# Second half's tokens normed one tile at a time during the first half and kept in DRAM, with inputs loaded and inner sums made at other steps, in a float32 decoder layer on one core

## The chip, the core and the metric

The kernel runs on one core of a Trainium2 chip. The metric is device time in microseconds (us), the median of three runs: 1939.29 us for the kernel before (1936.71 to 1942.11). Everything is float32. The engines are TensorE (PE in the profile; PEld is its weight load), VectorE (DVE), ScalarE (ACT), GpSimd (POOL) and SyncE (SP), which here issues nearly all the DMAs.

## What is computed

A decoder layer on 2048 tokens of width 512: attention with 32 heads of 128, cross attention to a small context, and a bias mixture of 64 experts, each behind a layer norm without weights and each added to its input. Only the first part matters here:

```python
def _layernorm(x, axis=-1, eps=1e-05):
    m = jnp.mean(x, axis=axis, keepdims=True)
    v = jnp.var(x, axis=axis, keepdims=True)
    return (x - m) / jnp.sqrt(v + eps)
...
q = (hidden_states @ Wq + bq).reshape(b, n, H, HD)
k = (hidden_states @ Wk + bk).reshape(b, n, H, HD)
v = (hidden_states @ Wv + bv).reshape(b, n, H, HD)
q = rmsnorm(q, gq)
k = rmsnorm(k, gk)
scores = jnp.einsum('bnhd,bmhd->bhnm', q, k) * scale
attn = jax.nn.softmax(scores.astype(jnp.float32), axis=-1).astype(q.dtype)
out = jnp.einsum('bhnm,bmhd->bnhd', attn, v).reshape(b, n, H * HD)
return out @ Wo + bo
...
x = x + _L0_attn_ref(_layernorm(x, axis=-1), ...)
```

There are 32 sequences of 64 tokens, so attention stays inside a sequence.

## The kernel before, in words

**Tokens.** The 2048 tokens are 16 tiles of 128 (NT), 8 pairs of tiles (NPAIR), 4 quads of 4 tiles (NQUAD), 2 halves of 8 tiles. A pair is an `AttentionInput` (L272): its constructor loads the two tiles (L283), `norm` (L285) takes their mean and variance (`statistics`, L216: L222 and L223 on VectorE for each tile, then the inverse root on ScalarE, L229 and L230, or on GpSimd, L226 and L227) and puts the two subtract-and-scale steps (L289, VectorE) on the list `waiting`. `turn` (L294) transposes the pair on TensorE into PSUM banks of the pool ps_s (three banks, which the scores, the mix and the sums of squares use too) and writes blocks for a Strassen product: three copies on ScalarE (L312 to L314), two sums on VectorE (L315, L316), two on GpSimd (L317, L318).

**Heads.** The 32 heads are 16 groups of two (NHG). The main loop (L1235) runs over 32 steps, for each half all 16 groups. The projections use Strassen's seven products in place of eight. In the first group of a half the two quads are handled one after the other (`single`, L1183, with `HeadGroup.project`, L419): these are the first and the second unit. In the 15 other groups both quads are taken together (`double`, L1194, with `Window`, L609): here Strassen's scheme is used twice, which needs, for each of seven outer products o, four more sums of the half's blocks: `inner_input` (L324), two on VectorE (L328, L329), then two on GpSimd (L330, L331). They are made once for each half.

**Weights.** `Weights` (L91) loads a group's Wq, Wk and Wv in six DMAs of 256 KB (L107). `prepare` loads those of the next group; their own Strassen sums (L120 on VectorE for the very first group, else on GpSimd; L152 to L155 on GpSimd) are made step by step by `make`.

**The order of the work.** Inside the attention part the orders of TensorE, VectorE, ScalarE and GpSimd are those of the program (`manual_schedule`, L67 and L1100): an instruction waits for all that the program put ahead of it on its engine. SyncE is not listed there; the framework orders its DMAs itself, except those of `load` (L212). The program is therefore a hand-written interleaving. `project` of a unit yields 14 times (steps 1 to 14), and `single` calls what is listed for a step (L1185, and the table `between` of the caller). A window has four groups n of outer products, (1, 5), (2, 6), (7, 3) and (4), with four steps m each, and `double` has a plan for each (n, m): `v` does a piece of the value projection, `line.scale` multiplies queries and keys of an earlier unit by their inverse root mean squares (L527 on GpSimd, L529 on VectorE; the factors come by a broadcast DMA, L518, into one of two buffers tagged rsb), `line.turn` and `line.attend` do scores, softmax (L254 to L262), mix (L577) and its store (L592, L599). Nearly each step also takes one entry from `waiting`.

**What TensorE waits for.** Products accumulate in PSUM banks. A partial result must be read by VectorE before the next product goes on in its bank: L445 and L450 in a unit, L651, L661 and L664 in a window (some by ScalarE, L654 and L388). Such a read is called a keep below.

**Where the norms and sums stand before the change.** At the start pairs 0 and 1 are loaded and normed; `turn` of each loads the pair two further on (L320). In the first group, `coming[0].norm()` (L1240) stands ahead of the first unit; pair 2 (in the second half 6) is turned after step 6 and pair 3 (7) after step 11. The second unit makes the inner sums 1 and 5 after steps 2 and 4, the first window 2, 6, 7, 3 and 4 after (0, 0), (0, 2), (1, 0), (1, 2) and (2, 1). In the last window of the first half pairs 4 and 5 are loaded into the two rsb buffers after (2, 1) and (2, 2), normed by `norms` (L1289) ahead of that window's last softmax, and turned after it.

## Time and profile before

| | |
|---|---|
| median of three runs | 1939.29 us |
| the profiled execution: its time | 1943.95 us |
| the profiled execution: its span, first to last instruction | 1942.2 us |
| mean granted TensorE clock | 0.989 |
| attention of the first half | 10 to 705 us |
| attention of the second half | 705 to about 1400 us |
| output projection, cross attention, experts | from about 1400 us |

The profile page lists busy time by engine, then the span in 40 slices, the DMA queues, the chain of work that ended last, and the costliest groups of instructions. A row of the timeline gives start, duration, engine, line of the kernel, operation, output and input; in brackets stands how long the engine had been idle before it, and what ended that. A DMA row (SPq) is the issue, not the transfer. The granted clock is TensorE's, as a share of full speed; the column DMA is the mean busy share of the 16 DMA engines.

Durations that recur, from the timeline: statistics of one tile L222 0.66 to 0.70 us and L223 0.18, inverse root on ScalarE 0.30 and 0.20, on GpSimd 0.23 to 0.43 and 0.71 to 0.86, subtract-and-scale L289 0.49 to 0.55, L328 0.37 to 2.00, L329 0.41 to 2.03, L330 0.72 to 1.18, L331 0.72 to 1.18.

### The profile page before, as it was taken

Reading aid. Unit: us, or ns where it says so; the run is one execution under the profiler, and the core shown is the slowest. Engines: PE = TensorE matmul, PEld = TensorE weight load, DVE = VectorE, ACT = ScalarE, POOL = GpSimd, SP = SyncE. Lnnn points to the kernel's source line nnn. Section 1 sums busy time; section 2 is a strip of 40 time slices with the busy share of each in tenths; the row PEclk is TensorE's granted clock in tenths of the full one; section 3 lists DMA queues with packets and bytes.
Section 4 is the critical chain, followed back from the end, with each engine's and each line's share of the span. In section 5 each row is a group of like instructions: output and inputs, shape, how many; then the busy total and the mean of one; then the engine's idle time right before and its main releaser. Section 6 shows DMA issues by size and latency. Waiting matters only on the chain.

```text
span 1942.2 us, 40532 instructions
## 1 busy us (share of the span) xinstructions
PE 1891.5 (97%) x16877; PEld 1628.0 (84%) x16877; DVE 1211.4 (62%) x2024; ACT 643.6 (33%) x1567; POOL 1046.5 (54%) x816
## 2 busy tenths in 40 slices
PE   8999999999999999999999999999998999999997
PEld 7888888888888878888888888888887888888875
DVE  5766767766667667766666666666545445554545
ACT  2244334344433443334433333443311112221122
POOL 4865667665567548666557666655225323332320
PEclk9999999999999999999999999999999999999998
DMA  4234333333433343333443333344933232223100
GB/s 132 66 99 129 123 111 109 110 99 117 131 125 100 109 141 101 101 107 99 127 133 113 110 109 100 99 130 135 300 118 128 90 106 70 69 90 112 49 20 22
DMA packets 162264, 210.72 MB, mean 108 GB/s; under 512 B 9888, under 2 KB 134880, under 8 KB 157984
## 3 DMA queue, kind: packets, MB, share of 16 engines
q1 hardware_dynamic: 160896, 207.05, 33.1%
q8 instruction: 133, 2.18, 0.5%
q10 hardware_dynamic: 1184, 1.08, 0.2%
q14 instruction: 51, 0.42, 0.1%
HBM read 169.82 MB, written 38.27 MB: 107 GB/s over the span
## 4 chain that ended last, share of the span: by engine, by line
PE 76%; DVE 11%; POOL 7%; issue 3%; DMA 2%; ACT 1%; SPq 0%; POOLq 0%; DVEq 0%; ACTq 0%
PE p_w L640 24%; PE py L822 18%; PE va L372 7%; PE vb L372 6%; POOL qk L719 5%; PE s L540 3%; PE ms_w L764 3%; PE o L577 3%; DVE qk L651 3%; DVE qk L664 3%; PE pa L430 1%; PE pt_p L246 1%; DVE qk L529 1%; DVE sums L259 1%; PE e_x L998 1%
## 5 line engine op out<-in xcount | busy, mean ns | idle before, releaser
L640 PE MATMUL p_w<-x,w 128*128 128x256 f32 x2940 | 726.0, 384 | 13.1 <-DVE qk L651 8.9
L640 PEld LDWEIGHTS p_w<-x,w 128*128 128x128 f32 x2940 | 522.3, 191 | 76.0 <-DVE qk L651 15.5
L651 DVE TENSOR_TENSOR qk<-p_w,qk 128x512 f32<-128x512 f32 x360 | 213.0, 599 | 148.6 <-PE p_w L640 113.0
L341 ACT ACTIVATE sq<-qk 128x512 f32<-128x512 f32 x256 | 158.2, 629 | 397.4 <-POOL qk L719 227.2
L372 PEld LDWEIGHTS va<-w,x 128*128 128x128 f32 x2048 | 265.3, 192 | 28.6 <-ACT v L388 18.3
L372 PE MATMUL va<-w,x 128*128 128x128 f32 x2048 | 277.2, 279 | 0.5 <-ACT v L388 0.5
L822 PE MATMUL py<-wo,a 128*128 128x256 f32 x1152 | 262.5, 381 | 0.0
L664 DVE TENSOR_TENSOR qk<-p_w,qk 128x512 f32<-128x512 f32 x360 | 219.7, 619 | 58.8 <-PE p_w L640 55.3
L120 POOL TENSOR_TENSOR w<-w 128x768 f32<-128x768 f32 x126 | 247.2, 1973 | 2.4
L822 PEld LDWEIGHTS py<-wo,a 128*128 128x128 f32 x1152 | 213.9, 190 | 35.6 <-issue 7.3
L262 POOL TENSOR_TENSOR prob<-prob,inv 128x512 f32<-128x512 f32 x64 | 76.7, 1198 | 293.5 <-DVE inv L261 292.5
L527 POOL TENSOR_TENSOR qk<-qk,rs 128x512 f32<-128x512 f32 x128 | 169.2, 1322 | 118.7 <-DMA rs<-row_w 98.6
L372 PEld LDWEIGHTS vb<-w,x 128*128 128x128 f32 x1536 | 202.3, 192 | 9.8
L372 PE MATMUL vb<-w,x 128*128 128x128 f32 x1536 | 203.3, 275 | 0.0
L388 ACT COPY v<-va 128x256 f32<-128x256 f32 x256 | 94.8, 370 | 320.5 <-PE va L372 320.4
L529 DVE SCALAR_TENSOR_TENSOR qk<-qk,gqk,rs 128x512 f32<-128x512 f32 x128 | 166.4, 1300 | 11.6 <-DMA rs<-row_w 10.2
L822 PE MATMUL py<-wo_t,a 128*128 128x256 f32 x608 | 142.2, 384 | 0.0
L822 PEld LDWEIGHTS py<-wo_t,a 128*128 128x128 f32 x608 | 114.6, 192 | 16.2 <-issue 0.8
L719 POOL TENSOR_TENSOR qk<-qk 128x512 f32<-128x512 f32 x60 | 90.3, 1504 | 60.6 <-DVE qk L664 58.2
L254 DVE TENSOR_REDUCE mx<-s 128x8 f32<-128x512 f32 x64 | 44.2, 691 | 110.0 <-PE s L540 110.0
L392 DVE TENSOR_TENSOR v<-vb,v 128x256 f32<-128x256 f32 x192 | 80.7, 420 | 47.9 <-PE vb L372 27.3
L592 ACT ACTIVATE ot<-o,bvt 128x256 f32<-128x256 f32 x256 | 99.2, 469 | 2.2 <-PE o L577 2.2
(177 smaller groups left out, 2191.4 us busy)
## 6 DMA issues: line engine op xcount, KB each, us to landing
rs<-row_w SPq DMA_DIRECT2D x120, 512.0 KB
mixed<-ot SPq DMA_DIRECT2D x64, 512.0 KB
a<-mixed SPq DMA_DIRECT2D x32, 1024.0 KB
w<-in_wq_dram SPq DMA_DIRECT2D x64, 256.0 KB
w<-in_wk_dram SPq DMA_DIRECT2D x62, 256.0 KB
w<-in_wv_dram SPq DMA_DIRECT2D x62, 256.0 KB
wo<-in_wo_dram SPq DMA_DIRECT2D x8, 1024.0 KB
x<-in_x_dram SPq DMA_DIRECT2D x28, 256.0 KB
```

Source lines behind the costliest of these rows:

```text
L120: on.tensor_tensor(*(it.rearrange("p c j d -> p (c j) d") for it in (out, a, b)), ALU.subtract)
L341: nc.scalar.activation(sq, of, AF.Square)
L372: nc.tensor.matmul(to[:, j, :], left[i][:, c, j, :], right[i][:, c, 2, :], start=first and j == 0 and c == 0, stop=c == 1, skip_group_chec ...
L388: nc.scalar.copy(self.v[h, ab], what)
L527: nc.gpsimd.tensor_tensor(k, k, rk, ALU.mult)
L529: lambda: nc.vector.scalar_tensor_tensor(q, q, gqk, rq, ALU.mult, ALU.mult)
L592: nc.scalar.activation(ot[:, h, :, b * SEQ : (b + 1) * SEQ], o[b][:, h, :, :], AF.Identity, bias=bvt[:, hg * HG + h : hg * HG + h + 1],)
L640: nc.tensor.matmul(bank[:, s, :], self.w.inner[o][i], inner_x[self.half, o][i], start=first and s == 0, stop=True, skip_group_check=True,)
L651: nc.vector.tensor_tensor(to(t, j), bank, add(t, j), ALU.add)
L664: nc.vector.tensor_tensor(to(t, j), bank, to(t, j), ALU.add)
L719: on.tensor_tensor(qk[to], qk[to], qk[what], ALU.add)
L822: nc.tensor.matmul(py, a[:, g, :], b[g // KH][:, g % KH, :], start=n == 0 and g == 0, stop=n == last and g == NHG - 1,)
```

## The change

Six things:

- A DRAM scratch `normed` holds eight normed tiles. In the first half's third to tenth group (2 to 9), a generator `normed_tile` loads one tile of the second half into a new buffer of its own after step (0, 0), takes its statistics after (0, 3), with the inverse root on ScalarE, and after (1, 2) subtracts and scales it and stores it to the scratch.
- Pairs 4 to 7 are loaded from the scratch; their `norm` does nothing, and `norms` with its step is gone.
- Pairs 2 and 3 are both loaded right after the first weights, into the two rsb buffers, and no longer by `turn` of pairs 0 and 1.
- The norm of pair 2 moves from ahead of the first unit to after its step 3.
- `inner_input` yields between its VectorE and its GpSimd part.
- In the second unit the two parts are called so: 1 after steps 1 and 2, 5 after 3 and 4, and the VectorE part alone of 2, 6 and 7 after 6, 8 and 12. In the first window: GpSimd's part of 2 at (0, 0), of 6 at (0, 1), VectorE's of 3 at (0, 2), GpSimd's of 7 at (1, 0), of 3 at (1, 1), VectorE's of 4 at (1, 2), GpSimd's of 4 at (2, 1). In the listing of the first window, the first call for an o that has not begun makes the VectorE part, the second the GpSimd part.

```diff
@@ -168,6 +168,9 @@
                     7: r[:, 0, 1, :],
                 }
 
+
+    normed = scratch.tile([NT // 2, P, D], F32, tag="normed", name="normed")
+
     def load_x(t, place=None):
         xt = xpool.tile([P, D], F32, tag="x", name=f"x{t}") if place is None else place
         nc.sync.dma_start(out=xt, in_=x_flat[bass.ts(t, P), :])
@@ -275,16 +278,27 @@
 
         def __init__(self, pair, beside=False):
 
-            self.pair, self.beside = pair, beside
+            self.pair = pair
             places = [None, None]
             if beside:
                 both = work.tile([P, 2, 2, QT], F32, tag="rsb", name=f"xs{pair}", bufs=2)
                 places = [both[:, i, :, :].rearrange("p h n -> p (h n)") for i in range(2)]
-            self.xs = [load_x(2 * pair + i, place) for i, place in enumerate(places)]
+            self.xs = []
+            for i, place in enumerate(places):
+                t = 2 * pair + i
+                if t < NT // 2:
+                    self.xs.append(load_x(t, place))
+                else:
+                    if place is None:
+                        place = xpool.tile([P, D], F32, tag="x", name=f"xn{t}")
+                    nc.sync.dma_start(out=place, in_=normed[t - NT // 2, :, :])
+                    self.xs.append(place)
 
         def norm(self):
 
-            for xt, (mean, rstd) in zip(self.xs, statistics(self.xs, f"a{self.pair}", self.beside)):
+            if self.pair >= NPAIR // 2:
+                return
+            for xt, (mean, rstd) in zip(self.xs, statistics(self.xs, f"a{self.pair}")):
                 waiting.append(
                     lambda xt=xt, mean=mean, rstd=rstd: nc.vector.tensor_scalar(
                         xt, xt, mean, rstd, ALU.subtract, ALU.mult
@@ -316,7 +330,7 @@
             nc.vector.tensor_tensor(s1, pt[1][:, 0:2, :], a22, ALU.add)
             nc.gpsimd.tensor_tensor(s2, s1, a11, ALU.subtract)
             nc.gpsimd.tensor_tensor(s4, a12, s2, ALU.subtract)
-            if pair + 2 < NPAIR // 2 or pair >= NPAIR // 2 and pair + 2 < NPAIR:
+            if pair in (NPAIR // 2, NPAIR // 2 + 1):
                 coming.append(AttentionInput(pair + 2))
 
     inner_x = {}
@@ -327,6 +341,7 @@
         x11, x21, x12, x22, s1, s2, s3, s4 = (it[:, bass.ts(k, QT)] for k in range(8))
         nc.vector.tensor_tensor(s1, x21, x22, ALU.add)
         nc.vector.tensor_tensor(s3, x11, x21, ALU.subtract)
+        yield
         nc.gpsimd.tensor_tensor(s2, s1, x11, ALU.subtract)
         nc.gpsimd.tensor_tensor(s4, x12, s2, ALU.subtract)
         inner_x[half, o] = {1: x11, 2: x12, 3: s4, 4: x22, 5: s1, 6: s2, 7: s3}
@@ -1116,6 +1131,7 @@
         )
     coming.append(AttentionInput(1))
     weights[0] = Weights("0_0", 0, (nc.sync, nc.scalar, nc.scalar))
+    coming.extend(AttentionInput(pair, True) for pair in (2, 3))
     load(g2[:, 0:1], gq.unsqueeze(1))
     load(g2[:, 1:2], gk.unsqueeze(1))
     load(bvt, bv_t)
@@ -1123,7 +1139,7 @@
     pt = ps_t.tile([P, 4, P], F32, tag="pt", name="pt_i")
     for i in range(28):
         nc.tensor.transpose(pt[:, i % 4, :], ident, ident)
-    for it in coming:
+    for it in coming[0:2]:
         it.norm()
     while waiting:
         take_waiting()
@@ -1180,6 +1196,14 @@
 
     line = Line()
 
+    def normed_tile(t):
+        xt = load_x(t, work.tile([P, D], F32, tag="xn", name=f"xn{t}", bufs=1))
+        yield
+        ((mean, rstd),) = statistics([xt], f"n{t}")
+        yield
+        nc.vector.tensor_scalar(xt, xt, mean, rstd, ALU.subtract, ALU.mult)
+        nc.sync.dma_start(out=normed[t - NT // 2, :, :], in_=xt)
+
     def single(unit, between):
 
         places = {6: [line.scale], 7: [line.turn], 11: [line.scale]}
@@ -1202,7 +1226,7 @@
             [[v], [v], [v, line.scale], [v]],
             [[v, line.scale], [v, line.turn], [v], [line.attend, line.scale]],
             [[v, line.scale], [v], [v], [v]],
-            [[v], [v], [v, line.turn], [*more.pop((3, -1), ()), end]],
+            [[v], [v], [v, line.turn], [end]],
         ]
         for (n, m), them in more.items():
             plan[n][m].extend(them)
@@ -1237,10 +1261,10 @@
         units = [HeadGroup(hg, 2 * half + t, w) for t in range(2)]
         prepare(n)
         if hg == 0:
-            coming[0].norm()
             single(
                 units[0],
                 {
+                    3: lambda: coming[0].norm(),
                     6: lambda: (coming.pop(0).turn(), coming[0].norm()),
                     11: lambda: coming.pop(0).turn(),
                 },
@@ -1250,16 +1274,24 @@
                 nc.vector.tensor_copy(bqd[:, :, 0::HG], b_0)
                 nc.vector.tensor_tensor(bqd[:, :, 1::HG], b_1, b_0, ALU.subtract)
                 nc.vector.tensor_scalar(gqk, g2[:, 0:1], g2[:, 1:2], HD**-0.5, ALU.mult, ALU.mult)
+            inners = {o: inner_input(half, o) for o in (1, 5, 2, 6, 7, 3, 4)}
+
+            def inner(o):
+                next(inners[o], None)
+
             sums_of_next(n)
             make(1)
             single(
                 units[1],
                 {
-                    2: lambda: inner_input(half, 1),
-                    3: lambda: make(1),
-                    4: lambda: inner_input(half, 5),
-                    6: lambda: make(1),
+                    1: lambda: inner(1),
+                    2: lambda: (inner(1), make(1)),
+                    3: lambda: inner(5),
+                    4: lambda: inner(5),
+                    6: lambda: (make(1), inner(2)),
+                    8: lambda: inner(6),
                     11: lambda: make(2),
+                    12: lambda: inner(7),
                 },
             )
         else:
@@ -1274,8 +1306,20 @@
                 more.setdefault((n, m), []).append(it)
 
             if hg == 1:
-                for at, o in (((0, 0), 2), ((0, 2), 6), ((1, 0), 7), ((1, 2), 3), ((2, 1), 4)):
-                    also(*at, lambda o=o: inner_input(half, o))
+                for at, o in (
+                    ((0, 0), 2),
+                    ((0, 1), 6),
+                    ((0, 2), 3),
+                    ((1, 0), 7),
+                    ((1, 1), 3),
+                    ((1, 2), 4),
+                    ((2, 1), 4),
+                ):
+                    also(*at, lambda o=o: inner(o))
+            if half == 0 and 2 <= hg < 2 + NT // 2:
+                norm = normed_tile(NT // 2 + hg - 2)
+                for at in ((0, 0), (0, 3), (1, 2)):
+                    also(*at, lambda norm=norm: next(norm, None))
             if (hg, half) == (NHG - 1, 0):
 
                 for m in range(2):
@@ -1286,13 +1330,6 @@
                     )
                     also(3, 3, lambda: coming.pop(0).turn())
 
-                def norms():
-                    for it in coming:
-                        it.norm()
-                    while waiting:
-                        take_waiting()
-
-                more[3, -1] = [norms]
             if n + 1 == len(groups):
                 four = four_blocks("wo_0")
                 wo_b = [[load_wo(k, 0, four[2 * k : 2 * k + 2])] for k in range(2)]
```

## The prediction, made before the changed kernel was run

> **What bounds the kernel now.** I read the page first: engine sums and chain of waits.
>
> ```profile
> PE 1891.5 (97%) x16877; PEld 1628.0 (84%) x16877; DVE 1211.4 (62%) x2024; ACT 643.6 (33%) x1567; POOL 1046.5 (54%) x816
> PE 76%; DVE 11%; POOL 7%; issue 3%; DMA 2%; ACT 1%; SPq 0%; POOLq 0%; DVEq 0%; ACTq 0%
> ```
>
> TensorE is the bound nearly everywhere; only time in which it idles, or runs at a lower clock, can be won. The busy-time table by stretches of 4 us finds those places (columns: stretch, then PE, PEld, DVE, ACT, POOL busy, granted clock, DMA share, GB/s):
>
> ```profile
> 16.00:20.00 4.00, 0.00 (x0) 0.00 (x0) 1.88 (x5) 0.21 (x1) 2.91 (x2) 0.91 0.67 244
> 20.00:24.00 4.00, 3.53 (x8) 2.86 (x9) 2.26 (x5) 1.18 (x4) 0.00 (x0) 0.50 0.02 4
> 76.00:80.00 4.00, 2.02 (x10) 1.82 (x11) 4.00 (x4) 0.58 (x1) 4.00 (x3) 1.00 0.00 0
> 696.00:700.00 4.00, 1.45 (x78) 1.25 (x72) 3.32 (x8) 1.11 (x3) 1.52 (x3) 1.00 0.80 250
> 700.00:704.00 4.00, 2.65 (x14) 2.44 (x15) 1.00 (x3) 2.96 (x9) 0.00 (x0) 0.74 0.62 205
> 780.00:784.00 4.00, 1.85 (x13) 1.55 (x11) 4.00 (x5) 0.00 (x0) 4.00 (x4) 0.98 0.00 0
> 784.00:788.00 4.00, 3.55 (x12) 3.20 (x13) 2.39 (x4) 1.11 (x3) 3.84 (x5) 0.50 0.00 0
> ```
>
> Four holes: first unit, first window of each half, turn of the halves. Elsewhere the windows are TensorE's own: from one window's sums of squares to the next it is 42.33 or 42.34 us almost without exception. The timeline tells what each hole waits for (the bracket is the idle before and who ended it):
>
> ```profile
> 12.75 1.81 SPq L173 DMA_DIRECT2D x<-in_x_dram  x4
> 18.05 0.69 DVE L222 BATCH_NORM_STATS2 st_a<-x 128x6 f32<-128x512 f32 x1 [4.05 <-DMA x<-in_x_dram]
> 20.47 3.75 PE L430 MATMUL pa<-x,w 128*128 128x256 f32 x8 [4.52 <-DVE qk L445]
> 73.28 3.76 POOL L120 TENSOR_TENSOR w<-w 128x768 f32<-128x768 f32 x2
> 73.37 2.00 DVE L328 TENSOR_TENSOR x<-x 128x256 f32<-128x256 f32 x1
> 75.30 2.02 DVE L329 TENSOR_TENSOR x<-x 128x256 f32<-128x256 f32 x1
> 77.97 1.99 PE L640 MATMUL p_w<-x,w 128*128 128x256 f32 x8 [2.02 <-DVE qk L651]
> ...
> 700.68 0.63 PE L246 MATMUL pt_a<-ident,xs 128*128 128x128 f32 x4 [3.22 <-DVE prob L255]
> 784.45 2.08 PE L640 MATMUL p_w<-x,w 128*128 128x256 f32 x4 [2.60 <-DVE qk L664]
> ```
>
> At 18 us VectorE stands on the third pair's input, with TensorE's keep (L445) queued behind; at 77 and 784 the keeps stand behind inner sums (L328, L329); at 700 the softmax (L254, L255), whose bank the transposes need, stands behind four norms.
>
> **Terms of the sum**, in the profiled execution (1943.95 us, span 1942.2 and 1.75 around it; 4.66 above the median 1939.29). Each hole is its stretch less the same work without a stall.
>
> *First unit.* From the first product (10.45) to the sums of squares (38.23): 27.78. The second half's second unit takes 22.15 (725.59 to 747.74); less 3.17 of squares, scores and mix and 0.44 of turned probabilities, plus two turns at 0.87, the work is 20.28. The hole is 7.5: 4.52 idle, some 3.0 of half clock. The change moves the norm to the third step and loads its input early. The DMA view has 5.31 MB in the first 22 us; less pair 3's 0.5, pair 2 landed as the last of 4.8 MB at 18.05. Now it is the last of 3.0; at that rate (some 0.305 MB/us from 2.3 on) it lands near 12, an estimate. Its 0.5 MB can hold the second half of the first weights back by 1.6 us; SyncE saw a first-weight load land at 10.7 and their sums started at 12.6, so that is just covered, and a longer delay would be paid one for one. The second weights fall behind 1 MB, 3.4 us later on SyncE's queue; POOL first reads them at 38.5, some 20 us after they land. The two buffers lent to the inputs are free after step 11, before the fetches that use them (42.5). The keep L445 then follows the weight sums (end 14.0), and product 6 runs at 15.95 without a stop. What is late next is the third pair's turn, wanted at 18.9: VectorE has L450 (to 15.8), two statistics 1.62, L392 0.42, tensor_scalar 0.54 (behind POOL's L120 until 18.9), L445 0.66, tensor_scalar 0.54, end near 20.6; less the first tile's transposes 0.44, idle 1.3. I take **-6.0**; ends -7.5 (nothing waits) and -2.8 (input no earlier than now: 2.7 idle and 2 of half clock).
>
> *First window, first half.* End of squares 58.94 to 101.88 is 42.94; a steady window has 40.03 (144.91 to 184.94), 1.09 of it a mix that this one lacks: hole 4.0. The vector parts of five sums were here; three (2, 6, 7) leave, 3 goes where 6 was (no stall there) and 4 where 3 was. At the old place of 7 POOL's L120 stays, but VectorE has nothing to lose to it. POOL's parts stay as many; those of 2 and 6 come a step or two earlier, while it waits for a fetch (4.13 idle before 70.11). The next window still waits 0.35 at its L664: **-3.5**, ends -2 and -4.
>
> *First window, second half.* 748.81 to 795.55 is 46.74 against 40.03: hole 6.7; idle 0.79 (behind 7) and 2.60 (behind 4), the rest half clock. Here a rule weighs. The Trainium skill, "TensorE: Matmul & The Clock Gate", Part 1, puts the clock to half after an idle window of about 3.4 us. By it a hole of 2.60 costs 2.60; the row after it shows a clock of 0.50, and at 77 us 2.02 cost none. By rule the term would be about 3.4 less a rest of 0.4, so -3.0, by row **-6.2**. I take the row; ends -3.0 and -6.7.
>
> *Turn of the halves.* Squares at 692.97 to 725.59: 32.62. Work: 22.15, plus 1.24 for the larger squares, plus four turns 3.48: hole 5.75. Gone are four statistics, four tensor_scalars and POOL's two short pairs. The scores end at 696.36, L254 and L255 (0.69 each) would end at 697.8, and the first transposes go there instead of at 700.68. Late next: the banks of the mix, freed by ScalarE's L592 (four, 1.55, begin 698.5 instead of 701.10), then the copies; the first product at 701.5 instead of 704.59, so -3.1, and 0.4 for its half clock. The remaining gaps are under 1 us each. **-3.5**; ends -2 (clock still drops) and -4.5. The norms of pairs 6 and 7 (705.9, 715.1) stalled no one: nothing. Four loads stay four, from the scratch.
>
> *Second units, both halves.* Three more vector parts each. L328 and L329 have medians 0.59 and 1.28, so 5.6 per unit; VectorE's idle is 7.5 of 20 (40 to 60), 6.0 (720 to 740), 7.0 (740 to 760). Behind the pair at step 6 is L445 of product 7, needed by product 4 at 742.40: it would end near 742.5 instead of 741.5. I take **+0.6** for both; ends 0 and +6. The rule that speaks against this change is here: the skill, "SBUF — State Buffer" (SBUF: two separate sides), says VectorE with two SBUF inputs and GpSimd take the shared ports for a whole instruction and the other blocks. The rows at 73 us agree: 2.00 and 2.02 beside L120, where 0.41 is common alone. All by that price, three pairs are 12 us, not 5.6, in 6 to 7.5 idle: +5 per unit. I take the medians, since L120 stands at steps 0 to 4, and the three pairs at 6, 8 and 12, where POOL has shorter pieces (L152 to L155, 1.0 to 1.28).
>
> *Eight windows, third to tenth.* Each gets 0.68 + 0.18 of statistics and 0.54 of tensor_scalar on VectorE, 0.30 + 0.20 on ScalarE, a load and a store of 256 KB on SyncE. In the window at 143 the statistics meet VectorE idle from 155.7 to 157.79, so nothing; ScalarE idles from 156.9 to 159.5, also nothing. The tensor_scalar meets 0.44 idle (165.65 to 166.09), is 0.1 too long, and by the port rule may wait out one POOL piece of 1.28; the keep it pushes (L651 at 169.33) has 0.75 until its product at 170.77. On SyncE the store waits for that tensor_scalar; behind it stands the mix's store of 170.81, whose buffer is needed a half window later. So 0 to 0.3 a window; **+0.8**, ends 0 and +2.4. The 4.2 MB more lie in queues that are a third busy. If that cover is gone, a window pays the full 1.4, +11.
>
> Sum: -6.0 - 3.5 - 6.2 - 3.5 + 0.6 + 0.8 = **-17.8**. From 1943.95: 1926.2; from the median: **1921.5**.
>
> **Rivals.** *Half of it comes back as a new wait.* The third pair's norm is late (-2.8), the turn waits on the mix's banks and the clock drops (-2), the window in the second half gives only -3.0, the rest -3.5, +0.6, +0.8: -9.9, 1929.4. For it: each of these waits is next in line. Against: each is shorter by the rows.
>
> *The sums only change place.* All moved pairs run at the port price, +10 for two units, and TensorE's clock drops after both, some 2 each: about -4, 1935. Against: POOL's long pieces are elsewhere.
>
> *Slower: the tile's load behind a waiting fetch on SyncE.* SyncE issues in order, and its third and fourth fetch wait for a buffer:
>
> ```profile
> 150.40 12.79 SPq L518 DMA_DIRECT2D rs<-row_w  x3
> ```
>
> The load is asked for before them, but the framework orders that queue. Behind the third (155.7) it lands 2.9 later (as the first load: 0.72 to 3.61), L651 comes 2.1 late against a slack of 0.9: 1.2 a window, still a gain. Behind the fourth (162.87), statistics hold VectorE to 166: 8.3 of stall and 2.3 of clock a window, +85, so about 2006. It decides from 2.2 a window. Against: in this trace loads without a pending wait go ahead of later ones (the seventh and eighth tile pairs' at 694, before the turns they follow in program).
>
> **How the numbers follow.** As reckoned 0.71 (1921.5); half back 0.17 (1929.4); only moved 0.07 (1935); slower 0.05 (2006). This kernel's measurement tells about 0.3% (5.8 us) from no change. The first two are faster, the third within, the fourth slower: 0.88, 0.07, 0.05. The range takes the best ends (-22.7, with scatter 1915) and the second case with its own (1931).
>
> **What would show it.** TensorE's wait at 20 us gone, its clock 1.00 through 16 to 28; first-window stretches near 39.4 and 40.5; the turn's stretch near 29; windows three to ten still 42.3, else the norms cost; in the second units no wait over 0.5 before L430. Wrong if the DMA wait before L222 stands again in the first unit or in the windows, if L328 and L329 average over 1.5 in the second units, or if the transposes at the turn wait longer for L592 than 1 us.

## The result, and the profile after

| | before | after |
|---|---|---|
| median | 1940.8 us (six runs, 1936.7 to 1943.7) | 1931.8 us (six runs, 1930.5 to 1933.6) |
| profiled execution (span) | 1943.95 (1942.2) | 1932.70 (1930.9) |

The ratio is 0.9954 (95% interval 0.9941 to 0.9966): 9.0 us faster, between 6.6 and 11.4. The forecast was -17.8 us, with a range of 1915 to 1931 us that the time missed by 0.8 us.

The engine sums and the chain on the page after:

```profile
PE 1887.6 (98%) x16877; PEld 1622.2 (84%) x16877; DVE 1228.4 (64%) x2024; ACT 646.8 (33%) x1579; POOL 1044.3 (54%) x812
...
PE 76%; DVE 12%; POOL 7%; issue 3%; DMA 1%; ACT 1%; SPq 0%; POOLq 0%; DVEq 0%; ACTq 0%
```

TensorE's busy time fell by 3.9 us with the same 16877 matmuls. VectorE's rose by 17 us with the same 2024 instructions: some of them now take longer. The busy-time table (columns as in the table of before) at the first unit, the turn and the first window of the second half:

```profile
16.00:20.00 4.00, 3.22 (x22) 2.85 (x21) 3.65 (x8) 1.50 (x4) 3.46 (x2) 1.00 0.77 263
20.00:24.00 4.00, 3.66 (x21) 3.11 (x21) 2.81 (x7) 1.02 (x3) 1.07 (x2) 1.00 0.01 4
...
692.00:696.00 4.00, 2.74 (x21) 1.98 (x18) 1.04 (x3) 3.55 (x11) 0.00 (x0) 1.00 0.76 231
752.00:756.00 4.00, 3.08 (x20) 2.71 (x19) 4.00 (x4) 0.63 (x2) 3.92 (x3) 1.00 0.00 0
...
776.00:780.00 4.00, 3.29 (x21) 2.80 (x22) 2.67 (x7) 2.64 (x6) 3.84 (x4) 1.00 0.00 0
```

None of these stretches has a clock under 1.00, and the wait of 4.52 us is gone. What is left before the third pair's turn (first two rows) and at the turn of the halves (last two; L607 is L592 of before) is short:

```profile
19.89 0.63 PE L249 MATMUL pt_a<-ident,xs 128*128 128x128 f32 x4 [0.78 <-DVE xs L303]
...
20.86 0.66 PE L249 MATMUL pt_a<-ident,xs 128*128 128x128 f32 x4 [0.34 <-DVE xs L303]
...
692.51 0.63 PE L249 MATMUL pt_a<-ident,xs 128*128 128x128 f32 x4 [0.47 <-PE o L592]
693.86 1.92 PE L249 MATMUL pt_a<-ident,xs 128*128 128x128 f32 x12 [0.71 <-ACT ot L607]
```

But at 752 and 776 TensorE idles 0.9 and 0.7 us, and GpSimd is busy nearly all through both. Two new waits, in the timeline after, whose line numbers are up to 15 above those of before (L120 is the same, L342 and L343 are the sums L328 and L329, L407 the values' addition L392, L460 the keep L445, L544 the scaling L529, L666 and L679 the keeps L651 and L664, L734 the addition L719). First half, the end of the first window:

```profile
86.08 0.73 POOL L345 TENSOR_TENSOR x<-x 128x256 f32<-128x256 f32 x1
...
86.89 0.73 POOL L346 TENSOR_TENSOR x<-x 128x256 f32<-128x256 f32 x1
...
87.57 2.94 POOL L734 TENSOR_TENSOR qk<-qk 128x512 f32<-128x512 f32 x2
...
87.71 1.68 DVE L734 TENSOR_TENSOR qk<-qk 128x512 f32<-128x512 f32 x1
88.88 0.63 ACT L356 ACTIVATE sq<-qk 128x512 f32<-128x512 f32 x1 [6.63 <-POOL qk L734]
89.41 0.35 ACT L403 COPY v<-va 128x256 f32<-128x256 f32 x1
...
89.82 0.38 PE L387 MATMUL va<-w,x 128*128 128x128 f32 x1 [1.11 <-ACT v L403]
```

Read from below: TensorE waits 1.11 us for a copy on ScalarE (L403), which stands behind a square (L356), which waited 6.63 us for GpSimd's addition (L734), which stands behind operand 4's two sums (L345, L346). Second half, the same window near its start:

```profile
750.58 3.93 POOL L120 TENSOR_TENSOR w<-w 128x768 f32<-128x768 f32 x2
750.82 2.02 DVE L343 TENSOR_TENSOR x<-x 128x256 f32<-128x256 f32 x1
...
752.77 2.29 DVE L544 SCALAR_TENSOR_TENSOR qk<-qk,gqk,rs 128x512 f32<-128x512 f32 x1
...
754.98 1.27 DVE L666 TENSOR_TENSOR qk<-p_w,qk 128x512 f32<-128x512 f32 x2
...
755.81 0.45 PE L655 MATMUL p_w<-x,w 128*128 128x256 f32 x1 [0.92 <-DVE qk L666]
```

Here the keep L666 is late, behind operand 3's second sum (L343, 2.02) and a scaling (L544, 2.29), both beside GpSimd's L120.

### The profile page after: what moved, and what is told of

It is laid out like the page before. It is cut to its first block, busy times and chain, and to the rows that moved or that the text cites. A ratio compares the mean times of both kernels' runs of the same rounds, so it can differ in the third digit from the quotient of the medians.

```text
span 1930.9 us, 40526 instructions
## 1 busy us (share of the span) xinstructions
PE 1887.6 (98%) x16877; PEld 1622.2 (84%) x16877; DVE 1228.4 (64%) x2024; ACT 646.8 (33%) x1579; POOL 1044.3 (54%) x812
## 3 DMA queue, kind: packets, MB, share of 16 engines
q10 hardware_dynamic: 1184, 1.08, 0.2%
## 4 chain that ended last, share of the span: by engine, by line
PE 76%; DVE 12%; POOL 7%; issue 3%; DMA 1%; ACT 1%; SPq 0%; POOLq 0%; DVEq 0%; ACTq 0%
PE p_w L655 24%; PE py L837 19%; PE va L387 7%; PE vb L387 6%; POOL qk L734 5%; PE ms_w L779 3%; PE s L555 3%; PE o L592 3%; DVE qk L666 3%; DVE qk L679 3%; DVE qk L544 1%; PE pt_p L249 1%; PE pa L445 1%; DVE sums L262 1%; PE py_x L1050 1%
## 5 line engine op out<-in xcount | busy, mean ns | idle before, releaser
L666 DVE TENSOR_TENSOR qk<-p_w,qk 128x512 f32<-128x512 f32 x360 | 213.0, 600 | 135.0 <-PE p_w L655 99.1
L356 ACT ACTIVATE sq<-qk 128x512 f32<-128x512 f32 x256 | 158.1, 629 | 400.2 <-POOL qk L734 225.4
L679 DVE TENSOR_TENSOR qk<-p_w,qk 128x512 f32<-128x512 f32 x360 | 220.1, 620 | 57.4 <-PE p_w L655 53.9
L120 POOL TENSOR_TENSOR w<-w 128x768 f32<-128x768 f32 x126 | 244.5, 1951 | 2.4
L542 POOL TENSOR_TENSOR qk<-qk,rs 128x512 f32<-128x512 f32 x128 | 172.4, 1347 | 113.1 <-DMA rs<-row_w 92.9
L403 ACT COPY v<-va 128x256 f32<-128x256 f32 x256 | 94.8, 370 | 308.9 <-PE va L387 308.7
L544 DVE SCALAR_TENSOR_TENSOR qk<-qk,gqk,rs 128x512 f32<-128x512 f32 x128 | 173.4, 1355 | 11.1 <-DMA rs<-row_w 10.0
L734 POOL TENSOR_TENSOR qk<-qk 128x512 f32<-128x512 f32 x60 | 90.7, 1511 | 61.1 <-DVE qk L679 58.7
L407 DVE TENSOR_TENSOR v<-vb,v 128x256 f32<-128x256 f32 x192 | 80.8, 421 | 45.6 <-PE vb L387 27.0
L607 ACT ACTIVATE ot<-o,bvt 128x256 f32<-128x256 f32 x256 | 99.2, 469 | 2.2 <-PE o L592 2.2
```

The lines of the kernel that those rows point to most:

```text
L120: on.tensor_tensor(*(it.rearrange("p c j d -> p (c j) d") for it in (out, a, b)), ALU.subtract)
L356: nc.scalar.activation(sq, of, AF.Square)
L403: nc.scalar.copy(self.v[h, ab], what)
L542: nc.gpsimd.tensor_tensor(k, k, rk, ALU.mult)
L544: lambda: nc.vector.scalar_tensor_tensor(q, q, gqk, rq, ALU.mult, ALU.mult)
L607: nc.scalar.activation(ot[:, h, :, b * SEQ : (b + 1) * SEQ], o[b][:, h, :, :], AF.Identity, bias=bvt[:, hg * HG + h : hg * HG + h + 1],)
```

## The experiments

The theory: the places and the turn were right, and the moved sums brought new waits in the first windows, some because VectorE pays GpSimd's time beside a sum (operand 3 above), some because GpSimd's own queue ends last (operand 4). The rivals: the sums gave what was forecast and another part gave less; or the hole sizes of the one profile were not typical.

The kernel before ran beside each set (medians 1939.55, 1941.44, 1939.91). A ratio here is to those runs, and microseconds "against before" are (ratio - 1) x 1940.

**The parts alone and left out in turn.** Six kernels; with before and after they are all eight combinations of three parts: start-up, normed tiles (eight norms and the turn), inner sums.

*Start-up alone*: before, with

```
+    coming.extend(AttentionInput(pair, True) for pair in (2, 3))
-            coming[0].norm()
+            if half:
+                coming[0].norm()
...
+                    3: lambda: half or coming[0].norm(),
```

> The kernel before with the start-up part alone (third and fourth pair loaded at once and normed at the third step). Forecast of this part: -6.0 us. Theory A (the parts' gains stand as the stretches of the changed kernel show them, and the shortfall lies in the inner sums): the stretch to the first sums of squares goes from 38.2 to 32.8 us, the second unit stays at 19.6, and nothing after it moves: -5.4 us against the kernel before. Rival B (the earlier finish is given back by the second unit, whose stretch grew from 19.64 to 20.90 in the changed kernel, because the weights of the next group and the fetch now come relatively later): the second unit grows to about 20.9 here too, in all -4.2 us.

*Normed tiles alone*: before, with `normed`, `normed_tile`, the loads from `normed`, and

```
+                for at in ((0, 0), (0, 3), (1, 2)):
+                    also(*at, lambda norm=norm: next(norm, None))
...
-                more[3, -1] = [norms]
```

> The kernel before with the normed tiles alone (eight windows norm one tile each and store it; the turn loads normed tiles). Theory A: the turn's stretch goes from 32.6 to 28.9 us, the windows stay at 42.34 and the second window at 40.7: -3.7 us. Rival B (the norm in the second window costs what that window lost in the changed kernel, 40.72 to 41.41): -3.1 us, with the second window near 41.4. If the prediction's price of 0.1 us a window held, the eight windows would sum to +0.8 and the whole to -2.9.

*Sums alone*: before, with the changed kernel's places and

```
         nc.vector.tensor_tensor(s3, x11, x21, ALU.subtract)
+        yield
         nc.gpsimd.tensor_tensor(s2, s1, x11, ALU.subtract)
```

> The kernel before with the inner sums alone moved (2, 6, 7 in the second unit, VectorE's and GpSimd's part a step or two apart). Theory A (VectorE pays up to 2 us for a sum beside GpSimd's long pieces, and GpSimd's own queue sets when the first window's additions start): the first windows take 42.0 and 44.0 us, the second unit of the first half about 1 us more: -4.5 to -5.8 us in all. Rival B (the holes were sized rightly, and the loss in the changed kernel comes from the other two parts): the first windows take 40.5 and 41.6, the second units stay: -9 us.

*The changed kernel without each part*: the same edits, taken back one at a time.

> The changed kernel without the start-up part. So far the parts alone gave -2.7, 0.0 and -0.1 us, the whole -9.0. Theory A (the parts add, each at its median alone): 0 us against the kernel before. Theory B (each execution draws its holes anew: the clock is halved in whole blocks of 3.41 us on a grid whose phase differs from execution to execution, and the first hole itself varies with the landing of the inputs; the parts' true means are nearer to their stretches, about -3, -3.7 and -4, and the medians alone were drawn high): -6 us against before, that is +3 against the changed kernel, and a spread of its times like that of before, since the first hole still draws.

> The changed kernel without the normed tiles (start-up part and sums stay). Theory A (the parts add at their medians alone): -2.8 us against before. Theory B (stretches): -5.3 us against before; the turn's stretch stays at 32.6 to 32.9 us, one halved block of 1.7 us in it in most executions.

> The changed kernel without the inner sums' part (start-up part and normed tiles stay). Theory A (the parts add at their medians alone): -2.7 us against before. Theory B (stretches): -6 us against before, the first windows at 43 and 46 to 47.8 us with one or two halved blocks in the second half's.

| start-up | normed | sums | ratio (interval) | against before |
|---|---|---|---|---|
| x | | | 0.9986 (0.9978 to 0.9993) | -2.7 |
| | x | | 1.0001 (0.9992 to 1.0010) | +0.2 |
| | | x | 0.9998 (0.9990 to 1.0006) | -0.4 |
| | x | x | 0.9982 (0.9974 to 0.9990) | -3.5 |
| x | | x | 0.9967 (0.9957 to 0.9978) | -6.4 |
| x | x | | 0.9970 (0.9960 to 0.9980) | -5.8 |
| x | x | x | 0.9954 (0.9941 to 0.9966) | -8.9 |

The three parts alone moved the stretches much as expected (32.87 us to the first squares; 28.87 at the turn, but 41.19 in the second window, as the rival said; 41.63 and 43.94 in the first windows and 20.87 in the second unit), but not the time: -2.7, +0.2 and -0.4 where the stretches asked for -5.4, -3.1 and about -5.

The parts alone sum to -2.9 and the whole is -8.9; but the pairs, which Theory A put at 0, -2.8 and -2.7, gave -3.5, -6.4 and -5.8. Theory A fell three times; of Theory B the last two came, the first is half of its -6. A single such ratio is uncertain by 1.4 to 2.4 us. Over the four pairs of kernels that differ in one part alone, the part is worth -5.0 (start-up: -2.7, -6.0, -6.0, -5.4), -2.1 (normed) and -2.7 (sums). The kernel before itself lay 1.9 us higher beside the pairs (1941.44) than beside the parts alone (1939.55); by the medians themselves, with 1940.24 for its 79 runs, the parts come to -4.9, -2.0 and -2.1.

The eight profiles say more than the medians. Each stretch, from one start of the sums of squares to the next, in the four kernels without the part that touches it and the four with it:

| stretch | part | without | with | mean change | forecast |
|---|---|---|---|---|---|
| to the first squares | start-up | 38.23, 37.55, 37.34, 36.09 | 34.29, 34.09, 32.87, 32.80 | -3.8 | -6.0 |
| second unit, first half | sums | 19.64 to 19.66 | 20.86 to 20.90 | +1.2 | +0.3 |
| first window, first half | sums | 44.01, 44.00, 43.15, 42.92 | 42.02, 41.83, 41.64, 41.34 | -1.8 | -3.5 |
| second window | normed | 40.38 to 40.99 | 41.19 to 41.63 | +0.7 | +0.1 |
| windows three to ten | normed | 42.34 | 42.34 | 0 | +0.7 |
| turn | normed | 32.61 to 32.86 | 28.87 | -3.8 | -3.5 |
| second unit, second half | sums | 22.15 | 22.15 | 0 | +0.3 |
| first window, second half | sums | 47.81, 46.63, 46.61, 46.18 | 43.94 to 44.00 | -2.8 | -6.2 |

Together -10.3, inside the interval of the medians. The profile of before had the longest stretch of four in the first unit and in both first windows: the third rival holds beside the theory. Each stretch is of one execution; that of the normed tiles alone was the fastest of its thirteen (1934.3 us, median 1940.9).

**Operand 4's GpSimd sums behind the additions**, in the changed kernel:

```
-                    ((2, 1), 4),
+                    ((2, 2), 4),
```

> The changed kernel with one edit: GpSimd's two sums of inner operand 4 stand behind its two additions at the same step of the window (a step later in the plan), not ahead of them. Theory A (GpSimd's queue is the bound there: in the changed kernel TensorE waits 1.11 and 0.95 us for a copy of the values that stands on ScalarE behind squares of those additions): the additions start about 1.5 us earlier, both waits go: -1.5 to -2.1 us against the changed kernel. Rival B (VectorE's addition at 1.68 us beside GpSimd's sets it, or the additions wait for VectorE's results anyway): the waits stay, 0. If inner operand 4 now comes too late for the third product of the last step, a wait for GpSimd appears at the end of the window, up to +1 us.

Measured 1930.0 us, ratio 0.9946 (0.9933 to 0.9958), 1.8 less than the changed kernel's median (the intervals overlap). The stretches settle it: the first windows fell from 42.02 to 40.53 and from 43.99 to 43.53. In its timeline

```profile
87.86 2.61 POOL L734 TENSOR_TENSOR qk<-qk 128x512 f32<-128x512 f32 x2
...
89.16 0.63 ACT L356 ACTIVATE sq<-qk 128x512 f32<-128x512 f32 x1 [5.19 <-POOL qk L734]
...
91.67 0.70 PE L655 MATMUL p_w<-x,w 128*128 128x256 f32 x2 [0.21 <-POOL x L345]
```

the waits for the copy are gone in both halves; what is left is 0.21 (0.42 in the second half) for operand 4 itself. In this execution the first unit took 35.12 instead of 32.80, so the clock stamps are 2.3 later: GpSimd's additions came about 2.0 us earlier in the window. Theory A holds.

**GpSimd's long pieces two steps later** in the second unit:

```
-                    2: lambda: (inner(1), make(1)),
+                    2: lambda: inner(1),
                     3: lambda: inner(5),
-                    4: lambda: inner(5),
+                    4: lambda: (inner(5), make(1)),
```

> The changed kernel with one edit in the second units: GpSimd's second pair of long weight sums (L120, 3.77 us in the profile after) is asked for at the fourth step, behind operand 5's sums, instead of at the second. Theory (the price of 1.84 and 2.03 us for operand 5's two sums in the first half is set by the GpSimd piece beside them, not by the sums): both take 0.4 to 0.7 us, as beside nothing, and the wait of 0.19 us at the next product goes. The long pair then stands beside operand 2's sums, which go from 0.81 and 1.48 to about 2.0 each and lengthen the wait of 0.65 behind them to 1.2 to 2.0: the unit, 20.90 us, gets 0 to 1 us longer. Rival (the sums are slow at that place for another reason): operand 5's stay at 1.8 to 2.0. The whole: 0 to +1.5 us against the changed kernel.

Ratio 0.9957 (0.9940 to 0.9974), no change that can be told. The rows decide. The changed kernel has for operand 5's sums

```profile
38.80 3.77 POOL L120 TENSOR_TENSOR w<-w 128x768 f32<-128x768 f32 x2
...
39.06 1.84 DVE L342 TENSOR_TENSOR x<-x 128x256 f32<-128x256 f32 x1
...
40.82 2.03 DVE L343 TENSOR_TENSOR x<-x 128x256 f32<-128x256 f32 x1
```

and this kernel for operand 5's and then operand 2's

```profile
40.81 0.41 DVE L342 TENSOR_TENSOR x<-x 128x256 f32<-128x256 f32 x1
...
41.15 0.42 DVE L343 TENSOR_TENSOR x<-x 128x256 f32<-128x256 f32 x1
...
42.91 3.76 POOL L120 TENSOR_TENSOR w<-w 128x768 f32<-128x768 f32 x2
...
43.43 1.57 DVE L342 TENSOR_TENSOR x<-x 128x256 f32<-128x256 f32 x1
...
44.93 2.02 DVE L343 TENSOR_TENSOR x<-x 128x256 f32<-128x256 f32 x1
```

The price goes with the GpSimd piece beside the sum, not with the sum: 0.41 alone, up to five times that beside L120. The wait behind operand 2 fell to 0.37 instead of growing, since VectorE came to operand 2 with its other work done: the unit took 20.17, 0.7 less. There I was wrong.

**The sums spread otherwise**, with the norms a window later; in the changed kernel:

```
-            if half == 0 and 2 <= hg < 2 + NT // 2:
+            if half == 0 and 3 <= hg < 3 + NT // 2:
...
-                    12: lambda: inner(7),
...
-                    ((0, 2), 3),
+                    ((0, 0), 3),
+                    ((0, 1), 7),
-                    ((1, 2), 4),
-                    ((2, 1), 4),
+                    ((2, 1), 4),
+                    ((2, 2), 4),
```

> The changed kernel with the moved work placed otherwise: the eight norms one window later (third window of the half is the first), inner operand 7's VectorE sums in the first window's second step instead of behind the second unit's last product, operand 3's at the first step, both where GpSimd still waits for its fetch; operand 4's at the third stage, GpSimd's two behind its additions. Theory (VectorE's sums cost 0.4 us each where GpSimd stands still and up to 2.0 beside its long pieces; GpSimd's queue bounds the first window): the first windows fall to about 40 and 42.5 us and the second window to about 41, -3 us against the changed kernel, -12 against before. Rival (the same sums meet another piece of GpSimd's at each place): no better than operand 4 alone, -1.8 against the changed kernel.

Ratio 0.9950 (0.9935 to 0.9965), no better than operand 4 alone. The second window fell to 40.35, so the norm there did cost the 0.7: in the changed kernel its tensor_scalar, beside L120,

```profile
114.61 4.05 POOL L120 TENSOR_TENSOR w<-w 128x768 f32<-128x768 f32 x2
...
117.17 1.77 DVE L1204 TENSOR_SCALAR xn<-xn,mv_n,rs_n 128x512 f32<-128x512 f32 x1
...
125.20 1.13 PE L655 MATMUL p_w<-x,w 128*128 128x256 f32 x4 [0.80 <-DVE qk L666]
```

took 1.77 us, where the seventh of the eight took 0.54; from there VectorE goes on with hardly a pause to the late keep L666. The first windows took 41.95 and 44.66: in the second half, operand 4's sums at (2, 1) put a wait of 1.54 before the next product (L679). The rival came true there.

**Operand 4's VectorE part back** at its place, in sums_spread:

```
-                    ((2, 1), 4),
+                    ((1, 2), 4),
```

> The changed kernel with the eight norms a window later, operand 3's and 7's VectorE sums in the first two steps of the first window, operand 4's where the changed kernel has them, and operand 4's two GpSimd sums behind GpSimd's additions. Theory: against the stretches of the changed kernel the first window of the first half goes from 42.0 to about 40.5, that of the second half from 44.0 to 42 (its waits of 0.92 and 0.95 gone, 0.42 and 0.4 left), the second window from 41.4 to 40.7: -4 us, about 1927.5. Rival (operand 4's VectorE sums or GpSimd's queue now meet another keep): 43 or more in the second half, -2 us.

Ratio 0.9947 (0.9934 to 0.9959), 1929.9 us: between theory and rival. First windows 41.31 and 42.86, second window 40.28. In the second half the wait of 0.92 behind operand 3's sums is gone with their move; one of 0.46 for a copy of the values and one of 0.28 for operand 4 remain.

**Operand 2's sums behind the second unit**, in sums_placed:

```
-                    6: lambda: (make(1), inner(2)),
+                    6: lambda: make(1),
+                    12: lambda: inner(2),
```

> The kernel of sums_placed with operand 2's VectorE sums behind the second unit's last product instead of at its sixth step. Theory: the wait of 0.65 us in the first half's second unit goes and the unit falls from 20.9 to about 20.2; the softmax behind the sums comes up to 1 us later, for which the first product of the window that needs its bank has room or pays 0.35: -0.3 to -0.7 us against sums_placed. Rival (the softmax is what the next window waits for): the wait of 0.35 us grows to over 1 us in both halves, +1 us.

Ratio 0.9943 (0.9930 to 0.9956), 1929.5 us, the lowest here, though its interval overlaps those of sums_placed and the changed kernel. The second unit fell from 20.87 to 19.96, the first window stayed (41.27), with a wait of 0.21 for the softmax's delay: in its stretch the unit won 0.9, a little more than expected.

**The cross-attention's weights earlier**, in sums_placed (the lines from `xw = work.tile` to the eight loads move up, and are not changed):

```
+    xw = work.tile([P, 4, P], F32, tag="xw", name="xw", bufs=1)
...
     (right,) = sums
     outs = {1: strassen_out(1, right, start_tail, a12)}
     next(outs[1])
-    xw = work.tile([P, 4, P], F32, tag="xw", name="xw", bufs=1)
```

> The kernel of sums_placed with the clearing and the eight loads of the cross-attention's weights ahead of the second output pair's loads. It is aimed at the part of the time that differs between executions of all these kernels: 552 to 555.8 us from the last sums of squares to the end, and in it a wait of 4.0 and one of 0.6 to 1.0 us for these weights, with one or two halved blocks of 3.41 us behind. Theory (the loads stand on SyncE's queue behind a load of the residual that waits for GpSimd's bias addition): both waits shrink under 1.7 us, no block is halved there, -5 to -8 us against sums_placed and a narrower spread. Rival (SyncE then issues the eight small loads, about 0.6 us each, ahead of the output's big ones, and the first products wait for those; or the buffer's memory comes free no earlier): 0, or up to +3 us.

Ratio 0.9959 (0.9947 to 0.9972), 2 us above sums_placed (the intervals overlap). The row shows the rival:

```profile
1458.68 3.75 PE L837 MATMUL py<-wo_t,a 128*128 128x256 f32 x8 [9.16 <-DMA a<-mixed]
```

The two waits became one of 9.16 for the output's first inputs, queued on SyncE behind the eight small loads; three blocks at half clock begin in it.

## Why the prediction was right and wrong

The direction, the four places and the turn were right. Of the size, 7.5 us of the -17.8 are missing from the stretches (-10.3). Two steps failed: each hole, with its half clock, was sized from one execution; and in the first windows the freed time was counted as won, with no new wait behind GpSimd's queue or behind a sum beside GpSimd. By the prediction's own terms:

- **Turn**, -3.5: right, -3.8, the same in all eight kernels. What came late next was as named: 0.47 for the mix and 0.71 for L607.
- **First window, second half**, -6.2: the step that failed most; -2.8. "I take the row", the prediction said of the half clock behind the 2.60 us. The row was right, but for one execution: two blocks at half clock stood there, and one in each of the other three profiles with the same wait. That is 1.0 of the 3.4 that are missing. The other 2.4 are the waits the prediction did not have: 0.42 for GpSimd's L542 (the pieces ahead of it, L152 and L153, take 1.46 and 1.34 beside the moved sums instead of 1.28 and 1.27), 0.92 behind operand 3's sums, 0.95 for the copy of the values.
- **First window, first half**, -3.5: -1.8. Before was 0.5 above the mean; about 1.2 are new waits (the 1.11 for the copy above all). The prediction looked at VectorE and said that GpSimd's parts "stay as many". They do, but the window had been stretched by VectorE's stalls; with these gone, TensorE arrives earlier and GpSimd's queue, busy almost without a gap from 66 to 95 us, is what ends last.
- **Second units**, +0.6: +1.2, all in the first half. This is the rule on the shared ports that the prediction weighed and set aside for medians of 0.59 and 1.28. In the first half the three moved pairs took 0.81 and 1.48, 1.52 and 1.48, 1.22 and 1.22, together 7.7 us against 5.6 by medians and 12 by the rule; and operand 5's, a step earlier and now wholly beside L120, 1.84 and 2.03 instead of 1.12 and 2.03. What the medians missed is that the pieces at those steps (L152 to L155) cost a sum 1.2 to 1.5 as well. Behind operand 2's sums stands a wait of 0.65, then come operand 6's:

```profile
48.27 1.99 PE L445 MATMUL pa<-x,w 128*128 128x256 f32 x8 [0.65 <-DVE qk L460]
48.81 1.28 POOL L154 TENSOR_TENSOR w<-w 128x512 f32<-128x512 f32 x1
48.85 1.52 DVE L342 TENSOR_TENSOR x<-x 128x256 f32<-128x256 f32 x1
...
50.05 1.45 POOL L155 TENSOR_TENSOR w<-w 128x512 f32<-128x512 f32 x1
...
50.30 1.48 DVE L343 TENSOR_TENSOR x<-x 128x256 f32<-128x256 f32 x1
```

The second half's three pairs took 7.8 us, and its unit had room for all of it.
- **First unit**, -6.0: -3.8. From the first product to the squares the forecast came (27.78 - 6.0 = 21.8; with the part 21.8, 22.2, 21.3 and 21.8 us), and the idle time before the third pair's turn was 1.12, forecast 1.3. What failed is the hole that it was taken from: without the part the other three executions take 25.1, 23.9 and 23.7 us there instead of 27.8, with waits of 2.0 to 3.2 us in place of 4.52 and one halved block or none in place of two. So the hole is worth -3.3 in the mean. The other 0.5 lies ahead of the first product, which comes at 10.5 to 13.6 us with or without the part, since the wait for the first tile and the clock behind it differ between executions (1.37 us at 9 us here, 2.55 in four_behind, with two blocks at half clock).
- **Eight windows**, +0.8: +0.7, but as one window's 0.7 instead of eight tenths: the number came by luck. The slow rival, a load behind a waiting fetch, did not come: each of the windows three to ten takes 42.34 us. It was not tried by itself.

The three parts by medians, -5.0, -2.1 and -2.7, against forecasts of -6.0, -2.7 and -9.1, say the same: the inner sums' term was more than three times too large. Of the rivals "half of it comes back as a new wait" gave the nearest time (1929.4), but named other waits; "the sums only change place" had the right mechanism at the price of a part of it.

Of the marks set down, the wait at 20 us, the turn and the windows came; the first windows (39.4 and 40.5 wanted from the end of the squares, 40.95 and 42.92 measured) and "no wait over 0.5" in the second units (0.65) did not. The mean of L342 and L343 there is 1.27 in the first half and 1.08 in the second, under the 1.5 that would have warned: a mean was the wrong mark. The wait of 0.19 stands behind operand 5's pair at 2.0; the 0.65 behind operand 2's at 0.81 and 1.48, to which VectorE came late (0.37 with operand 5's pair short, in pieces_later).

What stays open: the whole is 10.3 by stretches and 9.0 by medians, but the normed tiles and the sums, each alone, gave nothing by medians and about 3 us each by their stretches, which is outside their intervals; no run shows why. And the tail (from the last sums of squares to the end), which no part touches, differs between the eight profiles by 4.0 us (551.8 to 555.9).

## What the runs showed of the clock

The tail's difference, and much of the scatter, is one mechanism. Half clock comes in whole blocks of 3.41 us; within one execution their starts are whole multiples of 3.413 us apart (in the profile of before, those at 702, 783.9 and 1470 us lie 200, 224 and 425 blocks behind the one at 19.3), and from one execution to another the grid lies differently against the kernel. Of the eight tails, the four of 555.3 us or more have five such blocks that begin more than 16 us before the end, the four of 553.2 or less three or four.

Tables with one row for each block show what decides. The same wait of 2.60 us in before (rows 0.07 us behind its grid; on it the first two are 1.41 and 2.82), and in normed_alone:

```profile
780.50:783.92 3.42, 1.35 (x11) 1.10 (x9) 3.42 (x5) 0.00 (x0) 3.42 (x4) 0.99 0.00 0
783.92:787.33 3.41, 2.88 (x9) 2.53 (x10) 1.80 (x4) 0.89 (x2) 3.25 (x4) 0.50 0.00 0
787.33:790.74 3.41, 3.41 (x14) 3.05 (x13) 2.16 (x4) 1.23 (x2) 3.25 (x4) 0.51 0.00 0
```

```profile
774.00:777.41 3.41, 1.38 (x11) 1.14 (x9) 3.41 (x5) 0.00 (x0) 3.41 (x4) 1.00 0.00 0
777.41:780.83 3.42, 2.85 (x9) 2.49 (x10) 1.82 (x4) 0.86 (x2) 3.26 (x4) 0.50 0.00 0
780.83:784.24 3.41, 3.41 (x25) 3.20 (x24) 3.12 (x6) 2.26 (x5) 3.33 (x3) 1.00 0.00 0
```

A block with little TensorE work (1.41 on the grid, 1.38) is followed by one at half clock; after almost the same half-clock block (2.82 and 2.85) one execution took a second and the other not. And the same wait of 1.7 us in the tail, in after and in startup_alone:

```profile
1478.04:1481.45 3.41, 1.70 (x19) 1.43 (x19) 3.22 (x5) 2.06 (x12) 1.28 (x1) 1.00 0.00 0
1481.45:1484.86 3.41, 3.41 (x9) 2.72 (x9) 3.41 (x3) 0.00 (x0) 0.43 (x1) 0.50 0.00 0
```

```profile
1481.31:1484.72 3.41, 1.69 (x11) 1.19 (x11) 1.93 (x3) 3.35 (x18) 0.00 (x0) 1.00 0.00 0
1484.72:1488.14 3.42, 3.42 (x28) 3.02 (x27) 3.42 (x3) 0.00 (x0) 1.71 (x1) 1.00 0.00 0
```

In the fourteen profiles up to 1905 us, on the grid of the recorded clock changes, a full-clock block with 1.41 us of TensorE work or less was followed by half clock in all 33 cases, one with more than 1.72 in none, 73 of them with 2.6 or less, and between them in 15 of 32. So the border is near half of a block. A half-clock block was followed by another in all 17 cases with 2.82 us busy or less, in none of 45 with 2.95 or more, and in one of 4 between. As 2.85 us at half clock is the work of 1.4 at full clock, the border may be the same amount of work in both; that is an inference from these counts. So a wait spread over two blocks may cost nothing where the same wait inside one costs 1.7 us or 3.4. The Trainium skill, "TensorE: Matmul & The Clock Gate", Part 1, says that the window runs free of the kernel, which these runs agree with; but it asks for an idle window, and here half an idle one is enough.

Most of the spread goes with this: before ran from 1936.7 to 1945.9 us over all its runs, with mean clocks from 0.993 down to 0.987. In the 79 of them that ran beside the experiments, time and mean clock have a correlation of -0.80, which is 0.64 of the variance, at 1.2 us for each 0.001; the rest is not explained. The changed kernel, in six runs, ran from 1930.5 to 1933.6, at 0.992 to 0.994, as it would with fewer holes left to be drawn. The profile of before, at 0.989, was one of the dear ones.

## What to carry to other kernels

- A hole read from one profile is one draw. Price its idle time and its half clock apart, look at how far the profiled execution lies above the median (here 4.7 us; the first unit and the two first windows, whose holes were counted as gain, were 2.4 us longer than the mean of four kernels), and take the half clock at one block of 3.41 us unless several profiles show two.
- When a stall is removed, walk every queue through the new, earlier arrival: here GpSimd's queue and ScalarE's copies ended last once VectorE's stall was gone.
- VectorE's two-input sum costs what GpSimd does beside it (0.41 or 2.0 us here). Price each moved sum by the row that will stand beside it, not by the median of its line.
